# Layer 1 of a four-layer graph kernel: transposed rows copied by two engines, one operation moved ahead of the next group's matrices, two scalings moved into a later product

## The chip, the core and the metric

The kernel runs on one core of a Trainium2 chip. The core has a matrix engine (TensorE, PE in the profile, with its weight loads shown apart as PEld), VectorE (DVE), ScalarE (ACT), GpSimd (POOL) and a queue engine (SyncE, SP) that issues transfers. PE writes its results into PSUM, from which DVE and ACT read. The metric is the device time of one launch in microseconds, the median of three runs.

## The reference, cut to what matters

128 graphs of 64 nodes with 512 features go through four layers. Each ends with `x = layernorm(x + layer(x))`.

```python
# layer 0: two hypergraph convolutions with a relu and a layer norm between them
x = _layernorm(x + L0(x, adj, W1, b1, gamma, beta, W2, b2))
# layer 1: pairwise scores s_i + s_j, weighted by the adjacency
y = x @ w;  s = y @ a
A = s[..., :, None] + s[..., None, :]
A = tanh(A / 8) * 8;  A = where(A >= 0, A, 0.1 * A)
A = exp(A) * adj
A = A / sum(A, -1) * sum(adj, -1)
x = _layernorm(x + A @ x @ w)
# layer 2: three graph convolutions  adj @ (x W) + b, relu after the first two
x = _layernorm(x + L2(x, adj, W1, b1, W2, b2, W3, b3))
# layer 3: attention with 8 heads, adjacency and distance terms added to the weights
x = _layernorm(x + L3(x, mask, adj, adj, W_qkv, W_out, b_out))
```

Everything is fp32.

## The kernel before, in words

Two graphs make a pair (128 rows, one SBUF partition each) and four pairs make a group (`G = 4`, 512 rows); there are 16 groups. A group's rows lie in one tile `x` of 128 x 4 x 512. "Duo" 0 and 1 are the pairs 0, 1 and 2, 3.

**Matrix products.** `multiply` computes 512 x 512 by 512 x 512 with seven half-size products instead of eight (a Strassen-like scheme). `Left.sums` makes the sums of the left operand's quadrants on DVE (`s_...` in the profile), the weights' sums are made once and kept in DRAM. Each of the seven calls of `product` is four fp32 matmuls of 128x256, which the profile shows as eight records. Three accumulators are used: `a`, `b` and `c` in the profile, as in `a_q`, `b_q`, `c_q` for the product named q. The order is B11 into a, T1 into b, T2 into a, B21 into c, T3 into a, B22 into b, T4 into a. Between them ACT or DVE copies an accumulator away (`u_...`, L528 or L530), or DVE adds it to such a copy to make a quadrant of the result (L548 from c, L552 from a after T3, L556 from b). Since T4 goes on accumulating in `a`, it has to wait until L552 has read it. `last_add[key]` keeps the instruction of L556.

**Products with the adjacency.** `graph_T` multiplies rows by a 64 x 64 matrix of each graph and gives the result transposed: 64 matmuls of 64x64 per duo into two PSUM tiles `gt`, and then one copy of each tile by ACT into the transposed operand `aT` (L470). `agg` (L1045) multiplies by the adjacency without a transposition: per duo four matmuls of 64x512 into two tiles, which DVE adds to `x` (L1050). `gt`, `agg`, the score tiles `ss` and `den`, and the transposed rows `xtp` all come from one PSUM pool of four slots, `ps_gt`, handed out in turn.

**Order of the work.** Three groups are in work at once. `first_half` of group q (layers 0 and 1, prefix `a` in the order below) runs in step q, `second_half` (layer 2 and the first part of layer 3, prefix `b`) in step q + 1, and the rest (prefix `t`) in step q + 2. `load`, `rows` and `prep` prepare the matrices of the group of the next step. These functions are generators; a hand-written list of their `yield` names says in which order they are called:

```python
order = """
    t.v1 a.c1 t.v b.gt t.soft a.w1a1 a.w1a t.soft2 a.resid b.l2a1 b.l2a a.w1b1 t.ptp a.w1b t.pv a.lnh t.osum
    b.l2b1 a.c2a b.l2b a.c2b b.gb3 load a.w21 b.gh a.w2 rows b.l2c1 b.l2c2 a.ss b.l2c t.o1 a.den t.o2 a.c3 b.agg t.o
    a.p1 b.xT a.p2 b.q1 b.q t.ln3 b.k1 prep b.k b.dots
""".split()
```

Steps 1 and 16 have lists of their own. The list does not fix the order on each engine entirely: after the start, a scheduler places the instructions by itself, and `tc.issue_after(i)` (here through `behind(key)`) makes what is written under it come behind instruction i.

**The places that the change touches**, in the order of a step:
- `prepare` (L580 to L652) makes the matrices of the next group: L583 to L593 compare and sum, L618 multiplies the incidence by the edge weights (`hn`), L619 sums it (`db`), L599 to L601 invert, L625 and L627 make `dg` and `hb`. PE needs these only at `rbps` (L630).
- `first_half`: after layer 0 and its norm (L444 statistics, L445, L435 on ACT, L436, L448 scalings of the four pairs) L741 makes the scores `s4`, L745 spreads them on a diagonal, `e`. PE multiplies ones by it (`ss`), DVE and ACT make `t` out of it (L754 to L758), PE sums it (`den`), L767 and L768 divide. Then `graph_T` of layer 1 with `t` (`gt_l<-t,x`, copies into `aT_l`), the sums, the product with w (`l1w`), the addition to `x` (L784) and the norm of layer 1 (L444 to L448).
- `second_half`: the third product of layer 2 is `l2c` (around `ss` and `den` on PE), `agg` follows `gt_l<-t,x`, then the norm of layer 2, `xtp` with its copies, the products q and k of layer 3.
- `wo` is layer 3's output product of the group of two steps before; its seven products stand between `l2c`, `gt_l`, `agg` and `l1w`.

Of the kernel before, what the change touches and what calls it, by code (L numbers as in the profile page):

```python
# [11 lines left out]
ALU = mybir.AluOpType  # L12
AX = mybir.AxisListType

P = 128
C = 64
# [3 lines left out]
G = 4  # L20
# [21 lines left out]
def kernel(  # L42
# [59 lines left out]
    identc = const.tile([P, C], FP, name="identc")  # L102
# [33 lines left out]
    ten, vec, act = Engine(nc.tensor, PE), Engine(nc.vector, DVE), Engine(nc.scalar, ACT)  # L136
# [88 lines left out]
    class Weight:  # L225
# [63 lines left out]
        def scale(self):  # L289

            self.quads = []
            for u, raw in enumerate(self.raw):
                s = big.tile([P, 4, 2, Q], FP, name=f"{self.name}s_{u}", tag="big")
                b = {}
                for n, (k, m) in enumerate(((0, 0), (0, 1), (1, 1), (1, 0))):
                    for c in range(2):
                        f = (u * 2 + k) * 2 + c
                        act.mul(s[:, n, c], raw[:, n, c], ga_col[:, f : f + 1])
                    b[k, m] = s[:, n]
                    if n == 3:  # L300
                        self.quads.append(b)
                    if n % 2:
                        yield
# [20 lines left out]
    w_g = [Weight(t, 0, f"gw{'abc'[n]}") for n, t in enumerate((gW1, gW2, gW3))]  # L324
    w_q, w_k, w_v = (Weight(Wqkv, n * D, f"w{'qkv'[n]}") for n in range(3))
# [99 lines left out]
    def bcast(t, n):  # L425

        return t.unsqueeze(2).to_broadcast([P, n, C])
# [8 lines left out]
        vec.reciprocal(rs[:, at], rs[:, at])  # L436
        return rs

    def layer_norm(xg, key, pairs=range(G)):

        mv = small.tile([P, G, 2], FP, name=f"mv_{key}", tag="mv")
        for p in pairs:
            st = small.tile([P, 6], FP, name=f"st_{key}_{p}", tag="st")
            vec.bn_stats(st, xg[:, p, :])  # L444
            vec.bn_aggr(mv[:, p, :], st)  # L445
        rs = rstd(mv, G, key, slice(pairs[0], pairs[-1] + 1))
        for p in pairs:
            vec.tensor_scalar(  # L448
                xg[:, p, :], xg[:, p, :], mv[:, p, 0:1], rs[:, p : p + 1], ALU.subtract, ALU.mult
            )  # L450

    def graph_T(src, mat, dst, duo, key):

        ps = [ps_gt.tile([P, 4, 2, C], FP, name=f"gt_{key}_{duo}_{g}", tag="gt") for g in range(2)]
        for c in range(4):
            for p in range(2):
                for f in range(2):
                    for g in range(2):  # L460
                        rows, c0 = slice(g * C, (g + 1) * C), c * P + f * C
                        ten.matmul(  # L462
                            ps[g][f * C : (f + 1) * C, c, p, :],
                            src(2 * duo + p)[rows, c0 : c0 + C],
                            mat[rows, 2 * duo + p, :],
                            start=True, stop=True,
                        )
        o = dst[:, :, duo * Q : (duo + 1) * Q].rearrange("p c (a g i) -> p c a g i", a=2, g=2)
        for g in range(2):
            act.copy(o[:, :, :, g, :], ps[g])  # L470


    last_add = {}

    def behind(key):
        return tc.issue_after(last_add[key]) if key in last_add else nullcontext()
# [43 lines left out]
    def multiply(lefts, wt_q, dst, key, flipped=False, res=None, stops=(3,)):  # L520


        acc = [ps_acc.tile([P, 2, Q], FP, name=f"{n}_{key}", tag="acc") for n in "ab"]

        def snap(ps, m, n, what):
            t = work.tile([P, 2, Q], FP, name=f"{what}_{key}", tag="w")
            if res is None:
                act.copy(t, ps)  # L528
            else:
                vec.tensor_add(t, ps, res(m, n))  # L530
            return t

        pa, pc = acc
        product(pa, lefts, wt_q, B11, True, False, flipped)
        s1 = snap(pa, 0, 0, "u1")
        if 1 in stops:
            yield
        product(pc, lefts, wt_q, T1, True, False, flipped)
        s5 = snap(pc, 1, 1, "u5")
        if 2 in stops:  # L540
            yield
        product(pa, lefts, wt_q, T2, False, False, flipped)
        s2 = snap(pa, 0, 1, "u2")
        if 3 in stops:
            yield
        pb = ps_acc.tile([P, 2, Q], FP, name=f"c_{key}", tag="acc")
        product(pb, lefts, wt_q, B21, True, True, flipped)
        vec.tensor_add(dst(0, 0), pb, s1)  # L548
        if 4 in stops:
            yield  # L550
        product(pa, lefts, wt_q, T3, False, False, flipped)
        vec.tensor_add(dst(1, 1), pa, s5)  # L552
        if 5 in stops:
            yield
        product(pc, lefts, wt_q, B22, False, True, flipped)
        last_add[key] = vec.tensor_add(dst(0, 1), pc, s2).ins  # L556
        if 6 in stops:
            yield
        product(pa, lefts, wt_q, T4, False, True, flipped)
        if res is None:  # L560
            act.copy(dst(1, 0), pa)
        else:
            vec.tensor_add(dst(1, 0), pa, res(1, 0))

    def whole(gen):
        for _ in gen:
            pass

    def nat(t):

        return lambda m, n: t[:, 2 * m : 2 * m + 2, n * Q : (n + 1) * Q]

    def turned(t):

        return lambda m, n: t[:, 2 * n : 2 * n + 2, m * Q : (m + 1) * Q]


    def prepare(g):

        q, atc = g["q"], g["atc"]  # L580
# [3 lines left out]
        db = small.tile([P, 2, G], FP, name=f"db_{q}", tag="db")  # L584
        vec.reduce_sum(db[:, 1], ht, axis=AX.X)
        hn = grp.tile([P, 2, G, C], FP, name=f"hn_{q}", tag="hn", bufs=1)
# [9 lines left out]
        inv = small.tile([P, 2, G], FP, name=f"inv_{q}", tag="inv")  # L596

        def inverse(dst, src):
            vec.tensor_scalar_max(dst, src, TINY)  # L599
            vec.reciprocal(dst, dst)  # L600
            vec.scalar_tensor_tensor(dst, src, 0.0, dst, ALU.is_gt, ALU.mult)  # L601

        if q == 0:

            d_ps = [ps_gt.tile([P, G], FP, name=f"dps_{q}_{h}", tag="gt") for h in range(2)]
            for p in range(G):
                for h in range(2):
                    rows = slice(h * C, (h + 1) * C)
                    ten.matmul(
                        d_ps[h][rows, p : p + 1], ht[rows, p, :], atc[rows, p, 0:1], start=True, stop=True  # L610
                    )
            inverse(inv[:, 1], db[:, 1])
            for h in range(2):
                rows = slice(h * C, (h + 1) * C)
                inverse(inv[rows, 0], d_ps[h][rows])
        else:
            by_rows()
            vec.tensor_mul(hn[:, 1], hn[:, 0], g["wb"])  # L618
            vec.reduce_sum(db[:, 0], hn[:, 1], axis=AX.X)  # L619
            inverse(inv, db)  # L620
        cs = small.tile([P, G], FP, name=f"cs_{q}", tag="cs")
        g["cs"], g["rowsum"] = cs, rowsum

# [15 lines left out]
        for p in range(G):  # L639
            for h in range(2):  # L640
                rows = slice(h * C, (h + 1) * C)
                ten.matmul(s_ps[h][rows, p, :], ht[rows, p, :], hb[rows, p, :], start=True, stop=True)
        for h in range(2):
            rows = slice(h * C, (h + 1) * C)
# [31 lines left out]
    def first_half(g):  # L676
        q, xg = g["q"], g["x"]
        pair = lambda p: xg[:, p, :]

        left = Left(f"l0_{q}")  # L680
# [5 lines left out]
        for n in range(2):  # L686
            for i, _ in enumerate(multiply(
# [4 lines left out]
                stops=((2, 4), (2, 3))[n] if q == 1 else (3,),  # L692
# [18 lines left out]
        for m in range(2):  # L711
# [3 lines left out]
            rs = rstd(mv, 2, f"h_{q}_{m}")  # L715
# [26 lines left out]
                prod, xg[:, p, :], 1.0, wa_bc, ALU.mult, ALU.mult, accum_out=s4[:, p : p + 1]  # L742
            )
        e = grp.tile([P, G, C], FP, name=f"e_{q}", tag="e", bufs=1)
        vec.tensor_mul(e, identc.unsqueeze(1).to_broadcast([P, G, C]), bcast(s4, G))  # L745
        yield "w2"

        ss = ps_gt.tile([P, G, C], FP, name=f"ss_{q}", tag="gt")
# [20 lines left out]
        yield "den"  # L769
        left = Left(f"l1_{q}")  # L770
        for duo in range(2):
            graph_T(pair, t, left.t, duo, f"l1_{q}")
        yield "c3"
        with behind(f"wo_{q - 2}"):
            left.sums()
# [7 lines left out]
        for p in range(G):  # L783
            vec.scalar_tensor_tensor(  # L784
                xg[:, p, :], y[:, p, :], g["rowsum"][:, p : p + 1], xg[:, p, :], ALU.mult, ALU.add
            )
        layer_norm(xg, f"l1_{q}")
        yield "p2"


    def doubled(g):
# [194 lines left out]
    def second_half(g):  # L986
# [46 lines left out]
        h2.sums()  # L1033
        yield "gh"
        g3 = big.tile([P, G, D], FP, name=f"g3_{q}", tag="big")
        for n, _ in enumerate(multiply([h2], (w_g[2], q), nat(g3), f"l2c_{q}", stops=(3, 5))):
            yield f"l2c{n + 1}"
        yield "l2c"
        for duo in range(2):
            ps = [ps_gt.tile([P, D], FP, name=f"agg_{q}_{duo}_{p}", tag="gt") for p in range(2)]  # L1040
# [28 lines left out]
        left.sums()  # L1069
        yield "xT"  # L1070
        qT = big.tile([P, KD, T], FP, name=f"qT_{q}", tag="big")
        for _ in multiply([left], (w_q, q), turned(qT), f"q_{q}", flipped=True):
            yield "q1"
        with behind(f"q_{q}"):
            vec.tensor_add(xg, xg, bo_bc.unsqueeze(1).to_broadcast([P, G, D]))
# [179 lines left out]
    def attend(g, duo, pts, v, left):  # L1255
# [29 lines left out]
    order = """  # L1285
        t.v1 a.c1 t.v b.gt t.soft a.w1a1 a.w1a t.soft2 a.resid b.l2a1 b.l2a a.w1b1 t.ptp a.w1b t.pv a.lnh t.osum
        b.l2b1 a.c2a b.l2b a.c2b b.gb3 load a.w21 b.gh a.w2 rows b.l2c1 b.l2c2 a.ss b.l2c t.o1 a.den t.o2 a.c3 b.agg t.o
        a.p1 b.xT a.p2 b.q1 b.q t.ln3 b.k1 prep b.k b.dots
    """.split()

    step_1 = """
        b.l2a1 b.l2a a.lnh b.l2b1 a.c2a b.l2b a.c2b b.gb3 load a.w21 b.gh a.w2 b.l2c1 sumsq b.l2c2 a.ss b.l2c a.den b.agg
        a.c3 a.p1 b.xT sumsk a.p2 b.q1 b.q b.k1 rows b.k prep b.dots
    """.split()

    step_last = """
# [150 lines left out]
```

## Time and profile before

| | |
|---|---|
| median of three runs | 2797.4 us (2797.36 to 2798.42) |
| the profiled execution | 2797.6 us, its span 2795.8 us |
| granted TensorE clock | 1.00 over the whole span |
| one steady step (1036.03 to 1207.80) | 171.77 us |
| in it: PE, PEld, DVE, ACT busy | 171.4, 146.3, 123.8, 50.3 us |
| DMA share in it | 0.49 of 16 engines, 145 GB/s |

The profile is that of one execution. Times in it are microseconds from the start of the span, in the groups also nanoseconds. The steady step is read best in the timeline, which lists instructions by start: start, duration, engine, line, operation, what is written and read, shape, number of merged instructions, and in brackets the idle time before and what ended it. Lines with L are lines of the kernel before.

### The profile page before, as it was taken

Reading aid. Unit: us, or ns where it says so; the run is one execution under the profiler, and the core shown is the slowest. Engines: PE = TensorE matmul, PEld = TensorE weight load, DVE = VectorE, ACT = ScalarE, POOL = GpSimd, SP = SyncE. Lnnn points to the kernel's source line nnn. Section 1 sums busy time; section 2 is a strip of 40 time slices with the busy share of each in tenths; the row PEclk is TensorE's granted clock in tenths of the full one; section 3 lists DMA queues with packets and bytes.
Section 4 is the critical chain, followed back from the end, with each engine's and each line's share of the span. In section 5 each row is a group of like instructions: output and inputs, shape, how many; then the busy total and the mean of one; then the engine's idle time right before and its main releaser. Section 6 shows DMA issues by size and latency. Waiting matters only on the chain.

```text
span 2795.8 us, 67769 instructions
## 1 busy us (share of the span) xinstructions
PE 2769.4 (99%) x28870; PEld 2362.2 (84%) x28870; DVE 2000.2 (72%) x3858; ACT 818.3 (29%) x1469; POOL 38.1 (1%) x72
## 2 busy tenths in 40 slices
PE   9999999999999999999999999999999999999998
PEld 7878888888888888888888888888888888888887
DVE  6768687676776767767677676767767677676766
ACT  3222323232232223323223222332322323232232
POOL 2000000000000000000000000000000000000000
PEclk9999999999999999999999999999999999999999
DMA  8444455454544545445454454544545455454541
GB/s 255 162 136 145 129 158 145 133 163 130 166 130 140 161 132 166 122 141 165 124 168 130 139 161 136 155 130 143 162 127 163 129 148 152 126 163 127 154 122 61
DMA packets 309389, 405.15 MB, mean 145 GB/s; under 512 B 57409, under 2 KB 185185, under 8 KB 309089
## 3 DMA queue, kind: packets, MB, share of 16 engines
q1 hardware_dynamic: 304112, 385.05, 46.5%
q0 software_dynamic: 4976, 15.76, 1.5%
q8 instruction: 229, 3.75, 0.5%
q14 instruction: 72, 0.58, 0.1%
HBM read 369.78 MB, written 30.93 MB: 143 GB/s over the span
## 4 chain that ended last, share of the span: by engine, by line
PE 86%; DVE 7%; issue 4%; ACT 1%; DMA 1%; POOL 0%; SPq 0%; DVEq 0%; POOLq 0%
PE a_l0w L513 13%; PE b_l0w L513 7%; PE a_l2b L513 4%; PE a_q L513 4%; PE a_k L513 4%; PE a_v L513 4%; PE c_l0w L513 4%; PE a_l2a L513 4%; PE a_l1w L513 4%; PE gt_l L462 3%; PE a_wo L513 3%; PE a_l2c L513 2%; PE gt_l0h L462 2%; PE b_l1w L513 2%; PE b_l2b L513 2%
## 5 line engine op out<-in xcount | busy, mean ns | idle before, releaser
L513 PE MATMUL a_l0w<-w2w,aT_l0h 128*128 128x256 f32 x720 | 164.3, 381 | 0.0
L444 DVE BATCH_NORM_STATS2 st_l<-x 128x6 f32<-128x512 f32 x244 | 157.4, 671 | 0.1
L513 PEld LDWEIGHTS a_l0w<-w2w,aT_l0h 128*128 128x128 f32 x720 | 135.6, 190 | 18.8
L702 ACT ACTIVATE h<-h 128x1024 f32<-128x1024 f32 x58 | 61.3, 1057 | 216.6 <-DVE h L556 195.0
L448 DVE TENSOR_SCALAR x<-x,mv_l,rs_l 128x512 f32<-128x512 f32 x244 | 117.9, 540 | 1.8
L470 ACT COPY aT_l<-gt_l 128x512 f32<-128x512 f32 x176 | 90.4, 600 | 71.6 <-PE gt_l L462 71.5
L513 PE MATMUL b_l0w<-w2w,s_l0h 128*128 128x256 f32 x480 | 108.5, 379 | 0.0
L513 PEld LDWEIGHTS b_l0w<-w2w,s_l0h 128*128 128x128 f32 x480 | 90.1, 190 | 13.5
L1029 ACT ACTIVATE aT_h<-gth,gb_col 128x256 f32<-128x256 f32 x128 | 48.4, 489 | 159.0 <-PE gth L1021 159.0
L435 ACT ACTIVATE rs_l<-mv_l,eps_t 128x4 f32<-128x4 f32 (+1 forms) x64 | 19.0, 297 | 253.7 <-DVE mv_l L445 241.9
L513 PE MATMUL a_l2b<-gwbw,aT_h 128*128 128x256 f32 x360 | 86.6, 383 | 5.4 <-ACT aT_oT L1275 5.4
L513 PE MATMUL a_q<-aT_xT,wqw 128*128 128x256 f32 x360 | 86.6, 383 | 0.7 <-ACT aT_xT L1068 0.7
L513 PE MATMUL a_l2a<-aT_l,gwaw 128*128 128x256 f32 x360 | 86.5, 383 | 0.0
L513 PE MATMUL a_l2c<-gwcw,aT_h 128*128 128x256 f32 x360 | 85.3, 380 | 0.6 <-DVE g L552 0.6
L513 PE MATMUL a_l1w<-ww,aT_l 128*128 128x256 f32 x360 | 85.1, 379 | 0.0
L513 PE MATMUL a_k<-aT_xT,wkw 128*128 128x256 f32 x360 | 85.0, 379 | 0.0
L513 PE MATMUL a_l0w<-w1aw,aT_l 128*128 128x256 f32 x336 | 82.3, 388 | 0.0
L513 PE MATMUL a_l0w<-w1bw,aT_l 128*128 128x256 f32 x336 | 81.7, 379 | 0.0
L530 DVE TENSOR_TENSOR u_l0w<-a_l0w,b_bc 128x512 f32<-128x512 f32 x56 | 38.4, 686 | 59.8 <-PE a_l0w L513 59.8
L513 PE MATMUL a_v<-wvw,aT_xT 128*128 128x256 f32 x336 | 80.8, 383 | 0.0
L513 PEld LDWEIGHTS a_l2b<-gwbw,aT_h 128*128 128x128 f32 x360 | 67.2, 190 | 15.9 <-ACT aT_oT L1275 7.4
L513 PE MATMUL a_wo<-wow,aT_oT 128*128 128x256 f32 x336 | 79.5, 379 | 0.1
(531 smaller groups left out, 6471.1 us busy)
## 6 DMA issues: line engine op xcount, KB each, us to landing
w2w<-w2k SPq DMA_DIRECT2D x210, 256.0 KB, 2.7
x<-in_x_dram SPq DMA_DIRECT2D x15, 1024.0 KB, 6.7
w1aw<-w1ak SPq DMA_DIRECT2D x60, 256.0 KB, 2.7
w1bw<-w1bk SPq DMA_DIRECT2D x60, 256.0 KB, 2.6
ww<-wk SPq DMA_DIRECT2D x60, 256.0 KB, 2.8
gwaw<-gwak SPq DMA_DIRECT2D x60, 256.0 KB, 3.6
gwbw<-gwbk SPq DMA_DIRECT2D x60, 256.0 KB, 2.7
gwcw<-gwck SPq DMA_DIRECT2D x60, 256.0 KB, 2.7
```

What stands on the lines that cost most here:

```text
L435: act.activation(rs[:, at], mv[:, at, 1], AF.Sqrt, bias=eps_t)
L444: vec.bn_stats(st, xg[:, p, :])
L448: vec.tensor_scalar(xg[:, p, :], xg[:, p, :], mv[:, p, 0:1], rs[:, p : p + 1], ALU.subtract, ALU.mult)
L462: ten.matmul(ps[g][f * C : (f + 1) * C, c, p, :], src(2 * duo + p)[rows, c0 : c0 + C], mat[rows, 2 * duo + p, :], start=True, stop=True,)
L470: act.copy(o[:, :, :, g, :], ps[g])
L513: ten.matmul(acc[:, blk, :], lhsT, rhs, start=(first and blk == 0 and i == 0), stop=(last and i == n_k - 1), skip_group_check=True,)
L530: vec.tensor_add(t, ps, res(m, n))
L702: act.activation(hn, hn, AF.Relu)
L1029: act.activation(o[:, :, h, :], ps[h][:, c].rearrange("p (d a) i -> p d (a i)", d=2), AF.Relu, bias=gb2_col[:, k : k + 1],)
```

## The change: what it does

1. `graph_T` gets a switch `both`; with it the second of a duo's two PSUM tiles is copied by DVE and not by ACT. Only layer 1's calls in `first_half` set it.
2. The addition of `e` is remembered, and for groups from the third on L618, L619 and the inverses of `prepare` are placed behind the `e` of the group in work. In `second_half`, the part of `l2c` between its first two stops (which holds L548) is placed behind the same `e`.
3. The norm of layer 1 scales pairs 0 and 1 as before, and pairs 2 and 3 under a new stop `ln1`, which stands between the two parts of the product q and is placed behind L552 of that product (`q_{q-1}.d`). q stops after T3 (stop 5) and no longer after T2 (stop 3).

```diff
-    def layer_norm(xg, key, pairs=range(G)):
+    def layer_norm(xg, key, pairs=range(G), late=()):
...
-        for p in pairs:
-            vec.tensor_scalar(
-                xg[:, p, :], xg[:, p, :], mv[:, p, 0:1], rs[:, p : p + 1], ALU.subtract, ALU.mult
-            )
+        def scale(ps):
+            for p in ps:
+                vec.tensor_scalar(
+                    xg[:, p, :], xg[:, p, :], mv[:, p, 0:1], rs[:, p : p + 1], ALU.subtract, ALU.mult
+                )
+
+        scale(p for p in pairs if p not in late)
+        return lambda: scale(late)
...
-    def graph_T(src, mat, dst, duo, key):
+    def graph_T(src, mat, dst, duo, key, both=False):
...
         for g in range(2):
-            act.copy(o[:, :, :, g, :], ps[g])
+            if both and g == 1:
+                vec.tensor_copy(o[:, :, :, g, :], ps[g])
+            else:
+                act.copy(o[:, :, :, g, :], ps[g])
...
-        vec.tensor_add(dst(1, 1), pa, s5)
+        last_add[f"{key}.d"] = vec.tensor_add(dst(1, 1), pa, s5).ins
...
-            vec.tensor_mul(hn[:, 1], hn[:, 0], g["wb"])
-            vec.reduce_sum(db[:, 0], hn[:, 1], axis=AX.X)
-            inverse(inv, db)
+            with behind(f"e_{q - 1}") if q > 2 else nullcontext():
+                vec.tensor_mul(hn[:, 1], hn[:, 0], g["wb"])
+                vec.reduce_sum(db[:, 0], hn[:, 1], axis=AX.X)
+                inverse(inv, db)
...
-        vec.tensor_mul(e, identc.unsqueeze(1).to_broadcast([P, G, C]), bcast(s4, G))
+        last_add[f"e_{q}"] = vec.tensor_mul(
+            e, identc.unsqueeze(1).to_broadcast([P, G, C]), bcast(s4, G)
+        ).ins
...
-            graph_T(pair, t, left.t, duo, f"l1_{q}")
+            graph_T(pair, t, left.t, duo, f"l1_{q}", both=True)
...
-        layer_norm(xg, f"l1_{q}")
+        rest = layer_norm(xg, f"l1_{q}", late=(2, 3))
         yield "p2"
+        with behind(f"q_{q - 1}.d"):
+            rest()
+        yield "ln1"
...
-        for n, _ in enumerate(multiply([h2], (w_g[2], q), nat(g3), f"l2c_{q}", stops=(3, 5))):
-            yield f"l2c{n + 1}"
+        gen = multiply([h2], (w_g[2], q), nat(g3), f"l2c_{q}", stops=(3, 5))
+        next(gen)
+        yield "l2c1"
+        with behind(f"e_{q + 1}"):
+            next(gen)
+        yield "l2c2"
+        whole(gen)
         yield "l2c"
...
-        for _ in multiply([left], (w_q, q), turned(qT), f"q_{q}", flipped=True):
+        for _ in multiply([left], (w_q, q), turned(qT), f"q_{q}", flipped=True, stops=(5,)):
...
-        a.p1 b.xT a.p2 b.q1 b.q t.ln3 b.k1 prep b.k b.dots
+        a.p1 b.xT a.p2 b.q1 a.ln1 b.q t.ln3 b.k1 prep b.k b.dots
```

The list of step 1 gets `a.ln1` at the same place.

## The prediction, made before the changed kernel ran

> **What bounds the kernel now.** I read the page first (busy shares, chain), then who waits on the weight loads of the matrix engine (PEld), then the timeline of one steady step.
>
> ```profile
> PE 2769.4 (99%) x28870; PEld 2362.2 (84%) x28870; DVE 2000.2 (72%) x3858; ACT 818.3 (29%) x1469; POOL 38.1 (1%) x72
> ...
> PE 86%; DVE 7%; issue 4%; ACT 1%; DMA 1%; POOL 0%; SPq 0%; DVEq 0%; POOLq 0%
> ```
>
> PE is the bound. A gain can only be PE time spent waiting, and this hides in the busy share, because a matmul's modelled end covers a short gap. So I take it from differences of starts. A product of eight 128x256 records runs in 1.73 us (a_q 1089.71 to b_q 1091.43), 0.216 each; what exceeds this is a stall. One step is 171.77 us. The waits of the weight loads, longest first:
>
> ```profile
> PEld agg L1045 <- ACT aT_l L470: 12.3, 42, 0.3
> ...
> PEld a_l0w L513 <- DVE u_l0w L530: 9.6, 28, 0.4
> PEld ss L749 <- DVE e L745: 7.8, 15, 1.7
> ...
> PEld a_q L513 <- DVE qT L552: 5.3, 15, 0.4
> ```
>
> Columns: us in total, times, longest. The idle time includes what a load normally idles, so it overstates the loss; but three of these four rows are what the change touches. First e, in the timeline (start, us, engine):
>
> ```profile
> 1046.39 1.89 PE L513 MATMUL a_l2c<-gwcw,s_h 128*128 128x256 f32 x8
> ...
> 1047.53 0.41 DVE L618 TENSOR_TENSOR hn<-hn,wb 128x256 f32<-128x256 f32 x1
> 1047.86 0.41 DVE L745 TENSOR_TENSOR e<-identc,s 128x256 f32<-128x256 f32 x1
> ...
> 1048.33 0.70 PE L749 MATMUL ss<-e,bones 128*128 128x256 f32 x2
> ...
> 1048.87 0.59 PE L513 MATMUL b_l2c<-gwcw,s_h 128*128 128x256 f32 x2
> ```
>
> a_l2c takes 1.94 instead of 1.73 and ss 0.54 instead of 0.43: a stall of 0.21 and, behind it, 0.10 in which the load/multiply overlap refills. e ended at 1048.27; one operation of the next group (L618) stood ahead of it. Next the aggregation:
>
> ```profile
> 1059.24 2.05 ACT L470 COPY aT_l<-gt_l 128x512 f32<-128x512 f32 x4 [4.35 <-PE gt_l L462]
> ...
> 1059.94 0.59 PE L1045 MATMUL agg<-g,atc 64*64 64x512 f32 x1
> 1060.36 0.14 PEld L1045 LDWEIGHTS agg<-g,atx 64*64 64x64 f32 x2 [0.28 <-ACT aT_l L470]
> ...
> 1060.85 0.19 PEld L1045 LDWEIGHTS agg<-g,atc 64*64 64x64 f32 x2 [0.29 <-ACT aT_l L470]
> ...
> 1061.34 0.14 PEld L1045 LDWEIGHTS agg<-g,atx 64*64 64x64 f32 x2 [0.30 <-ACT aT_l L470]
> ...
> 1062.35 0.73 PEld L513 LDWEIGHTS c_wo<-wow,aT_oT 128*128 128x128 f32 x4 [0.81 <-issue]
> ```
>
> The four agg tiles take the four PSUM slots of the gt_l tiles, and ScalarE frees one each 0.48 us. agg lasts 2.42 us (1059.94 to c_wo at 1062.36). In the last step no gt_l stands ahead, and the timeline has agg from 2716.03 to b_wo at 2717.91: 1.88. So 0.54 is waiting. Last q:
>
> ```profile
> 1090.11 1.91 DVE L448 TENSOR_SCALAR x<-x,mv_l,rs_l 128x512 f32<-128x512 f32 x4
> ...
> 1091.43 1.89 PE L513 MATMUL b_q<-s_xT,wqw 128*128 128x256 f32 x8
> ...
> 1092.54 0.67 DVE L552 TENSOR_TENSOR qT<-a_q,u_q 128x512 f32<-128x512 f32 x1
> 1093.27 1.59 PEld L513 LDWEIGHTS a_q<-aT_xT,wqw 128*128 128x128 f32 x8 [0.35 <-DVE qT L552]
> ```
>
> The last a_q product accumulates onto the bank that L552 reads, and waits 0.11 (1093.27 against 1091.43 + 1.73), then 0.10 of refill (a_k at 1095.10).
>
> [...] ACT's u_l2c copy (1048.32, 0.59) and DVE's L548 (1048.53, 0.67) overlap at their usual lengths[...]. [...]
>
> **The change, part by part.** The instruction order of the changed program keeps PE's order but for two local swaps in the first two steps, and SP's queue with all DMAs is the same; only DVE and ACT move.
>
> *Copies on two engines.* Per step two 0.59 us copies leave ACT, two come to DVE. They fit in front of L1050, where DVE idles 2.66 us waiting for agg[...]. The changed program lets agg's first tile wait for ACT, its second for DVE. ACT's first copy starts 0.27 after the middle of the gt_l block (1058.03 + 0.94); I give DVE the same[...]. [...] I take 0.47 of the 0.54. The trace has no DVE copy from PSUM: between 0.54 (L448, SBUF only, gain 0.54) and 0.75 (L784, dearest 128x512 form, gain 0.40)[...]. 14 steady steps (2 to 15): 14 x 0.47 = 6.6 us, 5.6 to 7.5.
>
> *e ahead.* L618 goes behind e: e is 0.33 earlier, more than the 0.21. What is late next: the following a_l2c product overwrites the bank that ACT's u_l2c copy is still reading. The step at 2592.49 shows it: no next group, e early, ss on time, and the load of a_l2c waits 0.19 for ACT. From the a_l2c start to the six-record b_l2c it takes 4.40 there and 4.64 in the steady step. Gain 0.24; 13 steps have the stall: 3.1 us (2.6 if 0.04 more is lost, 4.1 if the ACT wait hides). The moved L618, L619 and the inverses are due only at rbps, 50 us later; the score chain behind ss has 0.5 us of slack (L758 ends 1053.54, den at 1054.05). Pinning L548 behind e costs nothing: it stood there.
>
> *Two scalings inside q.* Two of the four L448 (0.95 us) go behind L552, which then starts at once when its product is done (1091.65) and ends near 1092.35, 0.8 before it is needed. The two fit before L556 (1093.36, waiting for PE anyway). Their x rows are read next at 1125.05 (gt_l<-atc,x). Gain 0.21 x 14 = 3.0 us (2.6 to 3.0).
>
> *Step 1.* e stalls 1.45 there; the order puts it ahead of a 0.60 L548, and the copies end about 0.3 earlier before b_l1w's 0.3 stall: 0.8 (0.2 to 0.9).
>
> Sum 6.6 + 3.1 + 3.0 + 0.8 = 13.5 us, on a span of 2795.8 inside an execution of 2797.6, itself 0.2 above the median: 2797.4 - 13.5 = **2784**. The bounds added give 11.0 to 15.5, 2782 to 2786.5.
>
> **Rivals.**
> - *Taken back at xtp.* The layer-2 normalization (L448) ends at 1078.07, PE's transposes start at 1078.09 and need its last rows 0.57 later. If PE arrives 0.71 earlier and DVE does not follow, 0.17 + 0.1 is lost in each step, 3.8 us: 2787.7. Against: that DVE chain starts behind x<-b_wo, for which DVE waits on PE (1.03 idle), so it moves along.
> - *The aggregation gains nothing*, as another release is late at the same place (the copy held behind u_wo's addition at 1058.13): 6.9 us remain, 2790.5. Against: DVE is free at 1058.82.
> - *The DVE copies are slow*, slower than before. At length L the second pair frees its slot at 1059.30 + 2L, and agg needs 0.99 from there: 14 x (2L - 2.07) is lost, which beats the other 6.9 us from L = 1.28 us. At 1.5 us it gives 2803.5. For: 64-element runs written beside ACT into one tile. Against: the 128x512 DVE reads of PSUM shown in this step take 0.64 to 0.69.
> - *Nothing moves* (the order does not survive on the chip): 2797.
>
> **How the numbers follow.** Forecast 0.72, xtp 0.11, no gain at agg 0.09, slow copies 0.03, nothing 0.05. A measurement tells about 0.2% (5.6 us, 2791.8) from no change. Faster: 0.72 + 0.11 + 0.07 = 0.90; same 0.07; slower 0.03. The range 2781 to 2789 holds the forecast's bounds and the xtp rival.
>
> **What would show it.** agg near 1.95 us with a DVE copy ending by 0.7 us; ss on its 0.216 beat, with a small wait on ACT behind it; a_q without a wait on L552; a step of about 170.85 us. Wrong if DVE's copy exceeds 0.75, if agg stays at 2.4, or if a new PEld row of some us appears at xtp, den or b_l1w.

## The result, and the profile after

The changed kernel takes 2788.6 us (median of 8 runs, 2786.9 to 2789.9) beside 2797.3 us for the kernel before (8 runs, 2796.3 to 2798.4): a ratio of 0.9969, with a 95% interval of 0.9958 to 0.998. It is 8.7 us faster; 13.5 had been forecast, to 2784 us. Its profiled execution took 2789.5 us, of which the span is 2787.6.

First the waits of PE's weight loads in the changed kernel (us in total, times, longest), the rows that answer to those of before:

```profile
PEld agg L1067 <- ACT aT_l L480: 8.2, 14, 0.7
...
PEld xtp L1085 <- DVE x L451: 5.3, 16, 0.3
...
PEld ss L763 <- DVE e L757: 4.4, 14, 1.2
PEld a_l2c L523 <- DVE g L562: 3.9, 14, 0.8
```

The aggregation's row fell from 12.3 us in 42 waits to 8.2 in 14 (0.58 each, most of it agg's own pace, as its length below shows); the row of a_q behind DVE's qT is down from 5.3 us to one wait of 0.4; that of ss is shorter but not gone; and a_l2c behind DVE's addition L562 (L552 before; it was 1.0 us, once) is new. Read as before, from starts of matmuls, a steady step is 171.07 us instead of 171.77.

The aggregation, in the timeline (start, us, engine), with the copies of the transposed rows:

```profile
1055.29 0.58 ACT L480 COPY aT_l<-gt_l 128x512 f32<-128x512 f32 x1 [4.35 <-PE gt_l L469]
1056.23 0.58 ACT L480 COPY aT_l<-gt_l 128x512 f32<-128x512 f32 x1 [0.35 <-PE gt_l L469]
```
```profile
1055.34 0.69 DVE L478 COPY aT_l<-gt_l 128x512 f32<-128x512 f32 x1 [0.46 <-PE gt_l L469]
1056.27 0.69 DVE L478 COPY aT_l<-gt_l 128x512 f32<-128x512 f32 x1 [0.24 <-PE gt_l L469]
```
```profile
1056.00 0.59 PE L1067 MATMUL agg<-g,atc 64*64 64x512 f32 x1
1056.08 0.14 PEld L1067 LDWEIGHTS agg<-g,atx 64*64 64x64 f32 x2
...
1056.86 0.19 PEld L1067 LDWEIGHTS agg<-g,atc 64*64 64x64 f32 x2 [0.58 <-ACT aT_l L480]
1057.01 0.14 PEld L1067 LDWEIGHTS agg<-g,atx 64*64 64x64 f32 x2
...
1058.03 1.16 PEld L523 LDWEIGHTS c_wo<-wow,aT_oT 128*128 128x128 f32 x6 [0.81 <-issue]
```

agg lasts 2.03 us (1056.00 to 1058.03), 2.42 before. DVE's copy starts 0.05 after ACT's and takes 0.69, so the second agg tile of each pair comes 0.05 after the copy's end: 1055.34 + 0.69 + 0.05 = 1056.08, and again 1057.01.

Then e:

```profile
1043.68 0.08 DVE L753 DVE_READ_ACCUMULATOR xwa<-x,wa_bc 128x1 f32 x1
1043.79 0.42 DVE L757 TENSOR_TENSOR e<-identc,s 128x256 f32<-128x256 f32 x1
1044.13 0.42 DVE L630 TENSOR_TENSOR hn<-hn,wb 128x256 f32<-128x256 f32 x1
1044.27 0.30 PEld L763 LDWEIGHTS ss<-e,bones 128*128 128x128 f32 x2 [0.24 <-DVE e L757]
...
1047.54 0.68 DVE L562 TENSOR_TENSOR g<-a_l2c,u_l2c 128x512 f32<-128x512 f32 x1
...
1048.27 0.73 PEld L523 LDWEIGHTS a_l2c<-gwcw,aT_h 128*128 128x128 f32 x4 [0.25 <-DVE g L562]
```

e now stands ahead of the hn product, and ss starts on PE's beat. But e ends only 0.21 earlier than before, counted from the start of the a_l2c product in work (1.67 us after it instead of 1.88), not 0.33. It needs the last of the scores, which DVE reads out of its accumulator at 1043.68, and it starts 0.11 behind that start. In the kernel before, the hn product (L618, 1047.53) started together with that read and e 0.33 behind it:

```profile
1047.53 0.08 DVE L741 DVE_READ_ACCUMULATOR xwa<-x,wa_bc 128x1 f32 x1
```

So 0.21 of head start met a stall of 0.21 and left nothing over. The load of ss could be issued only as e ended, so the refill behind a late load (ss 0.54 us instead of 0.43) is still paid; and later the last a_l2c product waits in the same way for L562, another 0.10. The a_l2c product in between, which the forecast saw waiting for ACT's copy, doesn't wait (1045.24 to 1046.96, 1.73 us).

Last q, on VectorE:

```profile
1085.78 1.00 DVE L451 TENSOR_SCALAR x<-x,mv_l,rs_l 128x512 f32<-128x512 f32 x2
...
1087.31 0.69 DVE L562 TENSOR_TENSOR qT<-a_q,u_q 128x512 f32<-128x512 f32 x1
1087.91 1.00 DVE L451 TENSOR_SCALAR x<-x,mv_l,rs_l 128x512 f32<-128x512 f32 x2
1089.03 0.69 DVE L566 TENSOR_TENSOR qT<-b_q,u_q 128x512 f32<-128x512 f32 x1
```

Two scalings stand behind L562; it ends at 1088.00, and the product that goes on in that accumulator starts at 1088.83 without a wait.

Where the time went: the steady step gives 0.70 us. Yet single steps of this execution are longer than 171.07, by 0.95 (around 1227 us) and 1.73 us (around 1627); the kernel before has only one such excess, 0.20. Without these the spans differ by 8.25 + 2.68 - 0.20 = 10.7 us (9.9 from the first b_q on; the start of the program varies between profiles). These excesses I call irregular stalls. The page calls the idle time in them "issue", no semaphore ends it:

```profile
1625.81 1.94 PEld L469 LDWEIGHTS gt_l<-smat,x 64*64 64x64 f32 x123 [0.33 <-DVE sum L1214]
1629.03 0.20 PEld L469 LDWEIGHTS gt_l<-smat,x 64*64 64x64 f32 x5 [1.28 <-issue]
```

So there are two questions: why the regular gain is 10.7 and not 13.5, and what the irregular stalls are.

### The profile page after: what moved, and what is told of

It reads as the page before. It is cut to its first block, busy times and chain, and to the rows that moved or that the text cites. A ratio compares the mean times of both kernels' runs of the same rounds, so it can differ in the third digit from the quotient of the medians.

```text
span 2787.6 us, 67770 instructions
## 1 busy us (share of the span) xinstructions
PE 2760.6 (99%) x28870; PEld 2360.3 (85%) x28870; DVE 2021.5 (73%) x3888; ACT 805.1 (29%) x1439; POOL 38.1 (1%) x72
## 2 busy tenths in 40 slices
DMA packets 309388, 405.15 MB, mean 145 GB/s; under 512 B 57408, under 2 KB 185184, under 8 KB 309088
## 4 chain that ended last, share of the span: by engine, by line
PE 92%; DVE 2%; ACT 1%; issue 0%; DMA 0%; DVEq 0%
PE a_l0w L523 15%; PE b_l0w L523 7%; PE a_l2b L523 4%; PE a_q L523 4%; PE a_k L523 4%; PE a_v L523 4%; PE c_l0w L523 4%; PE a_l2c L523 4%; PE a_l2a L523 4%; PE a_l1w L523 4%; PE a_wo L523 4%; PE gt_l L469 3%; PE gt_l0h L469 2%; PE b_l2b L523 2%; PE b_q L523 2%; PE b_k L523 2%
## 5 line engine op out<-in xcount | busy, mean ns | idle before, releaser
L523 PEld LDWEIGHTS b_l0w<-w2w,s_l0h 128*128 128x128 f32 x480 | 90.1, 190 | 13.5
L480 ACT COPY aT_l<-gt_l 128x512 f32<-128x512 f32 x146 | 77.2, 597 | 80.2 <-PE gt_l L469 80.2
```

Source lines behind the costliest of these rows:

```text
L523: ten.matmul(acc[:, blk, :], lhsT, rhs, start=(first and blk == 0 and i == 0), stop=(last and i == n_k - 1), skip_group_check=True,)
```

## The experiments

All times below are medians with the range of runs; the kernels of one group shared the runs of the kernel before (2797.35, 2797.57 and 2797.23 us in the three groups).

### The three parts alone

**Copies alone.** The kernel before with

```diff
+            if both and g == 1:
+                vec.tensor_copy(o[:, :, :, g, :], ps[g])
+            else:
+                act.copy(o[:, :, :, g, :], ps[g])
```

> The kernel before with only the copies of layer 1's transposed rows split over ScalarE and VectorE. Theory A (the terms of the sum were mis-sized): the VectorE copy takes 0.69 us and starts some 0.04 us after ScalarE's, so agg falls from 2.42 to about 2.03 us, not 1.95: 14 x 0.385 = 5.4 us, and 0.3 in step 1: about 5.7 us faster than before, 2791.6. Rival B (the terms were right, the parts disturb each other): agg alone comes to 1.95 and the gain is the 6.6 us of the prediction, 2790.7 or less. Rival C (the irregular stalls of the matrix engine, some 3 us in the changed kernel's profiled execution, are brought by these copies): gain near 3 us, 2794.4, with stalls of about 1 us inside the gt_l blocks.

Measured 2791.57 us (2790.41 to 2795.54), 5.8 less than before (ratio 0.998, 0.9973 to 0.9988). The steady step is 171.38, 0.384 shorter, and no step of its profile has an irregular excess. Theory A: agg does not reach 1.95, with no other part beside it. C falls.

**e alone.** The kernel before with the hn product and the inverses behind e, and the two l2c additions behind e.

> The kernel before with only the order of e (the hn product and the inverses behind e, the two additions of layer 2 behind e). Theory A: the 0.21 before ss goes, its refill of 0.10 stays and the last a_l2c product waits 0.10 for the second addition (the line after the inverses): 0.11 per step, 13 x 0.11 + 0.6 in step 1, about 2.0 us, 2795.3. Rival B: 0.24 per step as predicted, 3.1 us + 0.5, 2793.8. Rival D (the new wait costs as much as the old one): no gain, 2797.3.

Measured 2794.81 us (2794.25 to 2797.28), 2.5 less (0.9993, 0.9984 to 1.0001: not told from no change by itself). The steady step is 0.096 shorter, not 0.24, with both waits in it; the waits of the weight loads:

```profile
PEld ss L752 <- DVE e L746: 4.4, 14, 1.2
PEld a_l2c L513 <- DVE g L552: 4.0, 14, 0.8
```

They are the two rows of the changed kernel, so they come from this part. One step, near 1630 us, has an irregular excess of 0.98. In step 1 the stretch of l2c ahead of ss takes 2.70 us instead of 3.18: 0.48. The profile shows A; by the medians alone it lies between A and B.

**q alone.** The kernel before with the two late scalings.

> The kernel before with only the two late scalings of layer 1 inside q. Theory A and rival B agree: 14 x 0.214 = 3.0 us, 2794.3, a_q to a_k without a wait. Rival C' (the irregular stalls come with this part): under 1.5 us gained, 2795.8 or more.

Measured 2794.03 us (2793.25 to 2796.23), 3.3 less (0.999, 0.9982 to 0.9999); the steady step is 0.216 shorter, all that was to be had. A and B. C' falls by the gain, though this profile has irregular stalls too, 1.2 us in two steps.

The steps add up: 0.384 + 0.096 + 0.216 = 0.696, and the changed kernel's is 0.698. The parts don't disturb each other in the regular steps. The profiles say the same of the whole program: from the first b_q on and without the irregular excesses, it is 5.3, 1.45 and 3.0 us shorter with one part each, 9.8 together, and 9.9 with all three. Yet the medians add up to 5.8 + 2.5 + 3.3 = 11.6 us and the changed kernel gains 8.7. Each of these gains is uncertain by some 2 to 3 us, so the gap of 2.9 alone would prove little.

### What is late behind e

VectorE is busy for 16.86 of the 17.00 us from 1032 to 1049 in the changed kernel, and no single gap there is longer than 0.04. If the two waits at e come from the amount of work there, it must be taken out, not reordered.

**All preparation behind L562.** The changed kernel with the next group's whole matrix preparation behind the second l2c addition (and `rows` moved behind `b.l2c` in the order):

```diff
+        later = (lambda: behind(f"l2c_{q - 2}.d")) if q > 2 else nullcontext
+        with later():
             vec.tensor_scalar(ht, atc, 0.0, None, ALU.not_equal)
...
+            with later():
+                by_rows()
```

> The changed kernel with all of the next group's matrix preparation (ht, its sum, the three row operations, the hn product, inverses, dg, hb, cs) behind the second addition of layer 2's third product, and traced after that product. Theory A: VectorE is the bound between the layer-0 output and that addition; with 1.1 us of preparation out of the normalization and 1.9 out of the stretch after e, ss loses its 0.10 refill and a_l2c its 0.10: 13 x 0.21 = 2.7 us less than the changed kernel, plus 0.5 in step 2: 2785.4. Rival E (ScalarE's u_l2c copy is next, as the prediction named it): a_l2c waits 0.1 to 0.2 for it and the gain over the changed kernel is 1.4 us or less, 2787.2 or more. Rival F (the preparation is late for the VectorE copies or for rbps): slower than the changed kernel, with new waits at agg or rbps.

Measured 2788.96 us (2787.14 to 2791.18): nothing gained. The step says why: 171.05, only 0.03 shorter, as three things stand against each other. ss and the last a_l2c product are on their beat (0.208 gained, A); the a_l2c product in between is 0.08 longer (E); and agg is 2.15 us instead of 2.03 (F), since the preparation now runs into the time of the copies: VectorE's begins at 1401.68, ScalarE's at 1401.44. Earlier in the same step VectorE waited 1.88 us ahead of L562:

```profile
1393.50 0.69 DVE L562 TENSOR_TENSOR g<-a_l2c,u_l2c 128x512 f32<-128x512 f32 x1 [1.88 <-PE a_l2c L523]
```
```profile
1401.61 0.15 DVE L668 TENSOR_TENSOR cs<-inv,deg 128x4 f32<-128x4 f32 x1
1401.68 1.42 DVE L478 COPY aT_l<-gt_l 128x512 f32<-128x512 f32 x2
```

**Tiles exchanged.** The changed kernel with `if both and g == 0`.

> The changed kernel with the two tiles exchanged: VectorE copies the first tile of each pair, ScalarE the second. Theory A (agg's second tile is late because the longer copy, 0.69 us, goes with the tile that is complete 0.04 us later): agg from 2.03 to about 1.98 us, 14 x 0.05 = 0.7 us, 2787.9. Rival H (it isn't the copy's length but VectorE's release that is slow): agg stays at 2.03 or grows.

Measured 2787.39 us (2785.83 to 2789.27); agg is 1.99 and the step 0.03 to 0.04 shorter. A by the trace; its 0.5 us are within the spread of the runs. Now both copies of a pair end together:

```profile
1397.39 0.69 DVE L478 COPY aT_l<-gt_l 128x512 f32<-128x512 f32 x1 [0.41 <-PE gt_l L469]
```
```profile
1397.43 0.59 ACT L480 COPY aT_l<-gt_l 128x512 f32<-128x512 f32 x1 [4.39 <-PE gt_l L469]
```

**Preparation into the gap.** With the tiles exchanged, the row operations go behind the addition of ss, into those 1.9 us, and only the rest behind L562 (`rows` stands behind `a.ss`):

```diff
+        hole = (lambda: behind(f"ss_{q - 1}")) if q > 2 else nullcontext
+        later = (lambda: behind(f"l2c_{q - 2}.d")) if q > 2 else nullcontext
...
+            with hole():
+                by_rows()
                 vec.tensor_mul(hn[:, 1], hn[:, 0], g["wb"])
+            with later():
                 vec.reduce_sum(db[:, 0], hn[:, 1], axis=AX.X)
```

> As e6_swap, and the next group's preparation split: its row operations (ht, hn, three sums, the hn product: 1.7 us) behind the addition of ss, in the 1.9 us in which VectorE waits for a_l2c; the second sum, inverses, dg, hb and cs behind the second l2c addition. Theory A (in e4 the preparation ran into the VectorE copies and cost agg 0.12 per step): ss and a_l2c keep their beat (0.21 less), a_l2c waits 0.08 for ScalarE's u_l2c copy, agg is 1.98: step 170.89 us, 0.18 x 13 = 2.3 us less than the changed kernel, 2786.3. Rival F (the VectorE copies stay late): step 171.0 and no gain, 2788.6.

Measured 2786.89 us (2784.86 to 2787.64; ratio to before 0.996, 0.9946 to 0.9974), the shortest of all. The step is 170.885, as A has it. In the timeline:

```profile
1386.93 0.60 PE L770 MATMUL ss<-e,bones 128*128 128x256 f32 x2
...
1387.13 0.58 ACT L538 COPY u_l2c<-a_l2c 128x512 f32<-128x512 f32 x1 [4.59 <-PE a_l2c L523]
...
1387.77 1.59 PEld L523 LDWEIGHTS a_l2c<-gwcw,aT_h 128*128 128x128 f32 x8 [0.21 <-ACT u_l2c L538]
```

ss has no wait left, and the load behind it waits for ACT's u_l2c copy: the wait that the forecast had named as next late. It costs 0.08.

### The irregular stalls

**The changed kernel again.**

> The changed kernel once more, unaltered, beside its variants. Theory A with instruction fetches (the steady step is 0.70 us shorter, which is the sum of the three parts, and what is missing of their 11.6 us is irregular: the matrix engine runs out of instructions when a fetch of its queue comes late, always at record 256k + 193 of its stream, and goes on about 1.5 us after that fetch has landed): step 171.07 us as before, total 2786 to 2790 with other or fewer stalls than in the first profile, each at 256k + 193. Rival G (the three parts disturb each other in a fixed way): stalls at the same two places, near 1227 and 1627 us, and of the same size, as in the first profile.

Measured 2788.86 us (2788.59 to 2789.89) in the second group, where the kernel with the preparation in the gap took 2786.89; the runs of the two don't overlap there. Its step is 171.08. It has stalls at 1227 and 1627 us again, and one at 2312 that the first profile had not: 3.2 us in all. G is right that places come back, wrong that they are fixed.

The changed kernel's page has this row among its DMA queues (packets, MB, share):

```profile
q8 instruction: 229, 3.75, 0.6%
```

Its trace has 229 packets of 16 KB in q8 and 58,680 records of PE, which are 57,740 loads and matmuls and 940 instructions of its sequencer: 256.2 records to a packet. So I took all of PE's records in order, numbered them from 0, and looked up each gap of over 0.4 us between two starts that no semaphore explains (from 200 to 2700 us, matmuls and loads of one block), with the last packet of q8 that landed ahead of it:

```
kernel            at us     gap us  next record   mod 256   after landing, us
changed           1226.78   0.95    26049         193       1.46
changed           1624.16   0.48    34241         193       1.49
changed           1627.67   1.36    34497         193       1.53
e alone           1630.28   0.98    34497         193       1.54
q alone            430.11   0.56     8897         193       1.37
changed, again    1226.58   0.53    26049         193       1.25
changed, again    1623.56   0.48    34241         193       1.22
changed, again    1627.06   1.09    34497         193       1.39
changed, again    2312.33   1.16    49089         193       1.36
prep. behind       428.04   1.30     8897         193       1.51
prep. behind      1058.83   2.23    22465         193       1.46
prep. in the gap   943.23   0.62    19905         193       1.32
prep. in the gap  1057.73   1.54    22465         193       1.33
tiles exchanged   1226.14   0.61    26049         193       1.35
tiles exchanged   1626.33   0.79    34497         193       1.36
```

Every one lies at the same place of the 256, and PE goes on 1.2 to 1.5 us after a packet has landed, as if it had run out of instructions. That these packets hold PE's instructions is my reading, from 256.2 records to a packet and from this table; the page names the queue, but not the engine that a packet is for. The profiles hold as many such places as packets, 229 (230 of both in one kernel below). Counted in order, and over all twelve profiles of this case, no such place starts less than 1.0 us after the landing of the packet one before it in the count; half of them start over 7.5 us after it, so by this reading most packets come in good time.

The longest stall, at 1058.83, cost more than its gap. Behind it the granted clock was 0.50 from 1062 to 1064 us and 1.00 again from 1065 on, and starts of the products lay 0.42 us apart and not 0.216: that step is 3.7 us longer than the others of its kernel. Behind the other long one, 2.12 us in a kernel below, the clock stayed at 1.00, so what lowers it is not shown.

**The stream shifted.** If that is so, more matmuls at the start move the places. The changed kernel with

```diff
+        if q == 0:
+            for n in range(64):
+                ten.matmul(rb_ps[:C, n % G, 0:1], ht[:C, n % G, :], atc[:C, n % G, 0:1], start=True, stop=True)
```

> The changed kernel with 64 more matmuls (128 records of loads and matmuls) near its start, into a tile that the next matmul overwrites. Theory A with instruction fetches: every irregular stall moves by half a fetch in the numbering of records, so that in this kernel's own numbering, pads included, it still lies at 256k + 193 and no longer at the matmuls where it lay (in the old numbering 256k + 65); step 171.07 us; total as the changed kernel plus 0 to 2 us for the pads. Rival G (something at those places of the program stalls): stalls at the old matmuls, in the own numbering at 256k + 65.

The test missed: 64 of these matmuls make 256 records, two matmuls and two loads each, so that the place in the count of 256 stayed. Measured 2801.57 us (2798.32 to 2804.66), as the pads hold up the start by 12.0 us. There is one packet more, 230. The stalls lie at 193 in its numbering (11713, 34753), and that at 34753 is the old 34497; both theories allow it. So once more with `range(32)`:

> As e8_shift, whose 64 matmuls came out as 256 records, a whole fetch, so that the boundary stayed where it was: now 32 matmuls, 128 records, half a fetch. Theory A with instruction fetches: irregular stalls lie at 256k + 193 in this kernel's own numbering, which is 256k + 65 in the old one, so at other matmuls than before; the long one at the old record 34497 (gt_l<-smat,x near 1627 us) is gone, others may come. Rival G (those places of the program stall): a stall of about 1 us at the old record 34497, which is 34625 here, 65 past a multiple of 256. The pads cost 12 us for 64 in e8_shift: some 6 here, total about 2794.5.

Measured 2797.03 us (2794.41 to 2798.46). The pads cost 4.9 us of the start, and the irregular excess of the steps is 5.4 us in its profile. Its gaps:

```
at us     gap us   next record   mod 256   after landing, us
 254.54   2.12      5057         193       1.39
 777.94   0.73     16321         193       1.63
 892.66   0.59     18881         193       1.29
2091.74   0.85     44481         193       1.23
```

The stalls at the old matmuls are gone, others have come, each at 193 of its own count: now in the middle of a gt_l block,

```profile
777.37 0.65 PEld L469 LDWEIGHTS gt_l<-smat,x 64*64 64x64 f32 x35
778.67 0.42 PEld L469 LDWEIGHTS gt_l<-smat,x 64*64 64x64 f32 x19 [0.65 <-issue]
```

where the changed kernel's stall at 1627 us lies 123 loads into its block. G is refuted: the stalls keep to record 193 of 256, not to a place in the program. Of the fifteen in the table, twelve lie in a block of 64x64 matmuls (gt_l) or right behind the aggregation that follows one. A gt_l block of 256 records takes 1.9 to 2.0 us; in the products of eight 256 records take some 28 us (1.73 us for 16). By my reading a packet that comes some microseconds late would be noticed first in a block.

**Without the adjacency loads.** Do small data packets hold those of q8 up? The changed kernel without the loads of the adjacency and masks of groups 3 to 15:

```diff
+        if q > 2:
+            nc.sync.dma_start(out=xg, in_=xsrc)
+            return dict(groups[2], q=q, x=xg)
```

> The changed kernel without the loads of adjacency and masks of groups 3 to 15 (they compute with group 2's): the instructions of the matrix, vector and scalar engines and their order are the same, the small packets of the DMA queues are mostly gone. Theory A with instruction fetches held up by the data queues: the irregular stalls shrink or go, and the time comes near the sum of the parts' regular gains, 2797.4 - 10.6 = 2786.8, with the steady step at 171.07. Rival K (it is the large weight transfers, or nothing in the data queues, that makes a fetch late): stalls of 2 to 3 us in all stay and the time is 2788.7.

Measured 2787.59 us (2786.83 to 2789.02), between the two expectations. Packets under 512 bytes fell only from 57,408 to 28,704, all packets from 309,388 to 280,682, less than I had thought. The stalls at 1227 and near 1627 us were gone but for 0.07, that at record 49089 was there with 1.41 us. As the stalls change from one execution to the next, one profile doesn't tell whether the loads mattered. Whether other transfers delay a packet stays open.

## Why the prediction was right or wrong

Direction and range held (2788.6 in 2781 to 2789, near its upper end); the sum of 13.5 us was too large by 4.8. That the range held is in part luck: the bounds of the sum itself, 2782 to 2786.5, don't hold the result, and the range had been drawn wider for a loss at xtp that did not come. About 3.2 of the 4.8 us are terms that were sized too large, and about 1.6 the irregular stalls, of which the forecast had nothing.

*Copies on two engines: right mechanism, 5.4 us instead of 6.6.* The steady step gives 0.384 instead of 0.47. The 0.47 was my estimate, between the gains of 0.54 and 0.40 that the forecast gives for copies of 0.54 and 0.75 us. VectorE's copy measured 0.69, inside those bounds and beside the 0.68 of L1050 in the kernel before. Its start, put at ScalarE's 0.27 after the middle of the block, is 0.05 later, as it takes the second tile; with the tiles exchanged it starts 0.04 ahead of ScalarE's (1397.39 and 1397.43). Exchanging the tiles won 0.04 of the 0.15 that agg is still above its unhindered 1.88. The rest has not been taken apart. VectorE did have the room: none of it was paid elsewhere. ScalarE and VectorE read their two tiles at the same time in 0.58 and 0.69 us, and ScalarE's copy is no longer than it was alone (0.59).

*e ahead: 1.3 us (13 x 0.096) instead of 3.1; here the working failed.* The forecast counted 0.33 of head start for e, the time from L618's start to its own, against a stall of 0.21, and took most of the refill behind it as gone too. It had left out what e itself waits for: e starts 0.11 behind the start of the read that brings its last score (0.11 to 0.13 wherever it follows that read directly), so the head start was 0.21. Nothing was left over for the next load to be issued ahead of time, and the refill of 0.10 stayed. And "what is late next" named ACT's u_l2c copy, by a step in which no preparation of a next group runs. In the steady step VectorE has that preparation between e and L562: L562 was now due earlier and came no earlier, which took another 0.10 back. Taking the preparation out of the way, in front of e and behind it, removed both waits (e then ends 0.6 ahead of ss), and then ACT's copy was next, at 0.08. So the copy was the third in line, not the first.

*Two scalings in q: right in mechanism and size.* 0.216 a step, 3.0 us; L562 ends 0.83 before it is needed, as forecast.

*Step 1: 0.65 instead of 0.8.* From the start of its a_l2c to its first b_q it takes 30.62 us instead of 31.27. With e alone this stretch is 0.42 shorter, with the copies alone 0.24. The totals can't show it, as the start of the program alone varies by a microsecond between profiles (27.7 to 28.7 us for its first 128 pp matmuls).

*The rivals.* xtp took nothing back: its loads wait 5.3 us for DVE and 0.7 with "issue", 4.6 and 1.3 before: the same sum. "No gain at agg", slow copies and "nothing moves" did not happen.

*What no step of the forecast had:* the irregular stalls of PE, each at record 193 of 256. By the steps, 5.4 + 1.3 + 3.0 + 0.65 = 10.3 us, or 10.7 from the spans, was gained regularly; the medians differ by 8.7. The two profiles of the changed kernel hold 2.7 and 3.2 us of irregular stalls, those of its parts none (copies), 1.0 (e) and 1.2 (q), that of before 0.2. This is enough for the missing 1.6 us. Whether the changed kernel is hit more often than its parts can't be told from so few profiles, and what brings a stall about is not shown.

## What to carry to other kernels

An operation that is moved ahead starts when its own inputs are there: look at what it waits for, not only at what it passes (e gained 0.21 us here, and not the 0.33 of what it passed). Where an engine is busy without a gap between two things that others wait for, a change of order helped only the first here (0.21 us of stall gone ahead of ss, 0.10 of new wait at the last a_l2c product); look at what it does until the second, and move work into a stretch in which the trace shows it idle (1.9 us ahead of L562). The release that is next late must be read from a step that has the same work on that engine. Give the longer of two parallel copies the tile that is complete first (0.69 beside 0.59 us: agg fell from 2.03 to 1.99). And when parts add up in the steady step (0.696 beside 0.698 us) but not in the total (11.6 beside 8.7), compare single steps with their median ahead of looking for an interaction.

## What was not expected of the hardware

In the traces PE's records outnumber the 16 KB packets of q8 by 256 to one (58,680 and 229), and every irregular stall looked up here lies at record 193 of the 256, the next record starting 1.2 to 1.6 us after a packet has landed. That PE ran out of instructions there is my reading. Twelve of the fifteen stalls in the table lie in a block of 64x64 matmuls or right behind the aggregation after one. The gaps were up to 2.2 us, and 0 to 5.4 us of a profiled execution of 2790 us went this way. Once the granted clock was 0.50 for some 3 us behind such a stall (1062 to 1064 us of the kernel with all preparation behind L562), and the step was 3.7 us longer than the others; behind the gap of 2.12 us it stayed at 1.00.

A matmul of 64x64 by one fp32 column makes two loads and two matmuls, and 64 of them took 13.7 us at the start (from 4.28 us to 18.00, 0.21 each); they held up the program by only 12.0, as PE had waited 1.7 us there before. The load of ss, issued just as e ended, cost 0.10 us behind it (ss 0.54 us instead of 0.43), although its matmul started on its beat (1044.27). On VectorE, e, which needs what the read of the accumulator brings, starts 0.11 to 0.13 us behind the start of that read, which itself takes 0.08.
